# Cross-attention on one Trainium2 core: two subtractions change places, a normalization is halved, stores change queues and the end is put in another order

## The chip, the core and the metric

The kernel runs on one core of a Trainium2 chip. The core has TensorE (PE; its weight loads are shown as PEld), VectorE (DVE), ScalarE (ACT), GpSimd (POOL) and SyncE (SP), which here only issues DMAs. The metric is the device time of one execution in microseconds. A ratio of two kernels is after over before.

## The reference

For each of 32 batches a cross-attention of 512 queries over 77 keys, with 20 heads of 32 columns, then an output projection, a bias and the residual. The reference also has three further key ranges (4, 4 and 16 keys), which are empty, since the context has exactly 77 rows. What is left of it:

```python
q = _heads(hidden_states @ to_q_w)                    # x: (32, 512, 640)
h_txt = _sdpa(q, _heads(ehs_txt @ to_k_w), _heads(ehs_txt @ to_v_w))   # context: (32, 77, 1024)
out = _merge(h_txt) @ to_out_w + to_out_b + hidden_states
```

`_sdpa` is softmax(q k^T / sqrt(32)) v in float32.

## The kernel before

Every product is made of float32 halves: an operand is split into a high part (a cast to fp32r, done by ScalarE) and a low part (operand minus high part, done by VectorE or GpSimd), and a product is high x high + high x low + low x high. Each operand so costs a cast and a subtraction, and each product three matmuls (`PAIRS`).

**Phases.** Up to about 260 us the kernel projects the context of all batches to keys and values, in groups of 512 context rows (the last, `LAST`, has 416), and keeps both parts in DRAM (`k_dram`, `v_dram`). Then come 160 slots, `slot(n)`: 32 batches of five chunks of 128 columns (four heads each), n = 5 b + j with chunk j. Then `end()`. The order on each engine is the order in which the code issues instructions; no scheduler moves them. An instruction waits for what it needs, and everything behind it on its engine or queue waits with it.

**A slot, by what it does.** Work of several chunks lies in one slot. For chunk n: `scores(n, t)` for t = 0 to 3, a tile of 128 queries each (three matmuls into one of three PSUM banks `sc`, then `nm`, the negated maximum, by VectorE), and `exps(n, t)` by ScalarE (four exponentials into `pn`, each with its sum). For chunk n+1: `queries` (15 matmuls into `pq`) and `split_q` (ScalarE casts `qt`, GpSimd copies two halves to the other partitions, L458, VectorE makes the low parts, L460); the next slot's scores read all three. For chunk n-1: `sums` (reciprocals, L506), `normalize` (GpSimd multiplies `pn`, L511) and `transpose_p` (VectorE transposes to `z`, L518, and SP stores it to DRAM, L525). For chunk n-3: `load_p` (SP loads the transposed probabilities as `raw`, L534 and L535). For chunk n-4 (`taken`), the probabilities are split and used:

- `cast_p`: ScalarE's two casts of `raw` into `pp`, 64 rows (L542) and 128 rows (L543);
- `last_p`: GpSimd's subtraction for the 64-row part (L556);
- `rest_p`: VectorE's subtraction for the 128-row part (L549);
- `values`: six matmuls into the PSUM tile `pa` (L570); the third and fourth read what `last_p` makes, the fifth and sixth what `rest_p` makes. There is one `pa`, so it must be free;
- `sum_a`: ScalarE copies the upper half of `pa` to `aw` (L581), VectorE adds it (L583).

For chunk n-5: `high_a` (ScalarE's cast of the attention's result into `at`, L590) and `low_a` (VectorE's subtraction, L595, the last that reads `pa`). And `piece`: the output projection of an earlier batch, matmuls `po` (L613), two pieces a slot; in chunk 3 the first piece reads the `at` that the same slot makes, in chunk 4 too. `finish` adds the residual (L642) and lets SP store it; `add_bias` (GpSimd, L606) adds the bias to a loaded residual. `split_x` and `transpose_x` prepare the next batch's x, in chunks 0 to 3.

**Keys.** `load_keys` puts a batch's keys into `kb`; `copy_keys` (GpSimd, L423 and L424) copies two parts of it, in chunk 1 for the second group of chunks and in chunk 4 for the next batch's first.

**Order by engine in a slot of the steady state, around the change.** GpSimd: `copy_keys` (chunks 1 and 4 only), `last_p`, `normalize`, the two copies of `split_q`, `add_bias`, the low parts of `split_x`. VectorE: `nm`, the reciprocals, `nm`, `rest_p`, `low_a` (in chunk 4 `low_a` comes before the second `nm`), `nm`, `split_q`'s two, `nm`, `transpose_p`, the two additions of `sum_a`. ScalarE: `cast_p`, `high_a` (in chunk 4 the other way round), eight exponentials, the cast of `split_q`, four, the copy of `sum_a`, four. TensorE: scores, queries, scores, queries, scores, first piece, `values`, scores, second piece.

**First slots.** Slots 0 to 7 have no projection yet (`has_out` is false; a batch's output starts one batch later), slots 0 to 2 make the last group's values beside, and the first `raw` is loaded in slot 3 (`LATE`). `filling` delays the refills of keys and values to behind `load_p` in slots that take a chunk but have no projection.

**The queue.** SP issues its DMAs in order. Each one holds one of eight semaphores until it has landed, so the ninth waits for the first.

## Time and profile before

| | us |
|---|---|
| three timed runs | 1936.98 median (1931.66 to 1938.36) |
| the profiled execution | 1923.57 |
| its span | 1921.7 |
| slot 0 begins | 262.2 |
| slot 10 begins | 365.6 |
| slot 159, the last, begins | 1864.3 |
| the last matmul ends | 1917.6 |

The steady state, in the order of costs, from the page's groups (line, engine, operation, out<-in, shapes, count, then busy time and mean ns of one, then the idle time of the engine before them and what ended most of it):

```profile
L549 DVE TENSOR_TENSOR pp<-raw,pp 128x1024 fp32r<-128x1024 f32 x160 | 261.1, 1632 | 31.0 <-ACT pp L543 24.9
L556 POOL TENSOR_TENSOR pp<-raw,pp 64x512 fp32r<-64x512 f32 x160 | 212.4, 1327 | 97.5 <-ACT pp L542 88.5
L511 POOL TENSOR_TENSOR pn<-pn,rs 128x1232 f32<-128x1232 f32 x160 | 503.5, 3147 | 23.8 <-DVE rs L506 12.3
```

A time in a timeline is that from the span's start; a row gives start, length, engine, line, operation, out<-in, shapes, how often in a run, and in brackets how long the engine was idle before it and what ended that.

### The profile page before, as it was taken

How to read it: one execution, taken by the hardware profiler on the slowest of the kernel's cores; microseconds unless marked ns; L12 is line 12 of the kernel's file. 1: busy time of each engine (PE TensorE's matmuls, PEld its weight loads, DVE VectorE, ACT ScalarE, POOL GpSimd, SP SyncE). 2: the span in 40 equal slices, each digit the busy share in tenths (PEclk: the TensorE clock that was granted, in tenths of full speed). 3: DMA queues.
4: the chain of work that ended last, by engine and by line, in shares of the span. 5: the costliest groups of instructions: out<-in, count | busy, mean ns of one | idle time of the engine just before them, and what ended most of it. 6: DMA issues, size and time to landing. Idle time of an engine off the chain costs nothing.

```text
span 1921.7 us, 37548 instructions
## 1 busy us (share of the span) xinstructions
PE 1883.1 (98%) x10332; PEld 1665.2 (87%) x10332; DVE 1626.7 (85%) x2494; ACT 1526.3 (79%) x6210; POOL 1422.3 (74%) x1116
## 2 busy tenths in 40 slices
PE   9999997999999999999999999999999999999998
PEld 7888886888888888888888889888888888888887
DVE  5444447899999989999999999999999999999985
ACT  3232247998998989899888899998998989999882
POOL 1100067888898888888888888888888888888873
PEclk9999998999999999999999999999999999999999
DMA  9878869898888888888989898898889888889875
GB/s 185 201 195 249 200 176 222 215 233 238 235 232 233 233 216 231 233 231 228 238 223 236 236 239 234 232 237 231 234 228 233 225 240 234 237 232 229 226 211 157
DMA packets 565022, 431.36 MB, mean 224 GB/s; under 512 B 191120, under 2 KB 473168, under 8 KB 564816
## 3 DMA queue, kind: packets, MB, share of 16 engines
q1 hardware_dynamic: 560304, 414.47, 84.0%
q0 software_dynamic: 4416, 14.34, 2.2%
q8 instruction: 85, 1.39, 0.3%
q14 instruction: 121, 0.99, 0.2%
q10 hardware_dynamic: 96, 0.16, 0.0%
HBM read 247.17 MB, written 181.64 MB: 223 GB/s over the span
## 4 chain that ended last, share of the span: by engine, by line
PE 44%; ACT 15%; DVE 14%; DMA 13%; issue 5%; SPq 5%; POOL 3%; DVEq 0%; POOLq 0%; ACTq 0%
PE pq L443 11%; PE po L613 11%; PE pv L191 6%; DMA raw<-pd 6%; ACT pn L496 6%; PE pk L191 6%; PE pa L570 5%; PE sc L478 4%; DVE pp L549 4%; DMA xs<-in_x_dram 3%; ACT pp L543 2%; DVE nm L486 2%; DVE z L518 2%; ACT xt L264 2%; ACT aw L581 2%
## 5 line engine op out<-in xcount | busy, mean ns | idle before, releaser
L496 ACT ACTIVATE pn<-sc,nm 128x77 f32<-128x77 f32 x2560 | 794.0, 333 | 32.6 <-DVE nm L486 27.7
L613 PE MATMUL po<-wo_s,at 128*128 128x320 f32 x3840 | 636.1, 314 | 7.3 <-DVE at L595 3.0
L443 PE MATMUL pq<-xt,wq_s 128*128 128x512 f32 x2400 | 621.4, 400 | 0.0
L613 PEld LDWEIGHTS po<-wo_s,at 128*128 128x128 f32 x3840 | 569.0, 189 | 15.9 <-DVE at L595 12.3
L496 ACT ACTIVATION_READ_ACCUMULATOR pn<-sc,nm 128x1 f32 x2560 | 545.7, 213 | 0.0
L511 POOL TENSOR_TENSOR pn<-pn,rs 128x1232 f32<-128x1232 f32 x160 | 503.5, 3147 | 23.8 <-DVE rs L506 12.3
L443 PEld LDWEIGHTS pq<-xt,wq_s 128*128 128x128 f32 x2400 | 429.9, 190 | 75.7
L478 PEld LDWEIGHTS sc<-kb,qt 128*128 128x128 f32 x1920 | 327.9, 189 | 59.7 <-POOL qt L458 12.1
L478 PE MATMUL sc<-kb,qt 128*128 128x154 f32 (+1 forms) x1920 | 317.9, 274 | 13.8 <-POOL qt L458 8.9
L486 DVE TENSOR_REDUCE nm<-sc 128x4 f32<-128x308 f32 x640 | 288.4, 451 | 44.1 <-PE sc L478 37.6
L549 DVE TENSOR_TENSOR pp<-raw,pp 128x1024 fp32r<-128x1024 f32 x160 | 261.1, 1632 | 31.0 <-ACT pp L543 24.9
L556 POOL TENSOR_TENSOR pp<-raw,pp 64x512 fp32r<-64x512 f32 x160 | 212.4, 1327 | 97.5 <-ACT pp L542 88.5
L570 PE MATMUL pa<-pp,vb 128*128 128x512 f32 x960 | 265.5, 407 | 10.0 <-DVE at L595 6.2
L518 DVE STREAM_TRANSPOSE z<-pn 128x1280 f32<-128x1280 f32 x160 | 241.9, 1512 | 8.0 <-DMA pd<-z 2.8
L583 DVE TENSOR_TENSOR pa<-pa,aw 64x512 f32<-64x512 f32 x320 | 222.7, 696 | 21.1 <-ACT aw L581 10.8
L460 DVE TENSOR_TENSOR qt<-pq,qt 64x512 fp32r<-64x512 f32 x320 | 219.2, 685 | 23.6 <-ACT qt L454 17.0
L265 POOL TENSOR_TENSOR xt<-xs,xt 128x512 fp32r<-128x512 f32 x160 | 202.6, 1292 | 34.0 <-ACT xt L264 30.7
L570 PEld LDWEIGHTS pa<-pp,vb 128*128 128x128 f32 x960 | 171.8, 190 | 57.8 <-DVE pp L549 13.2
L606 POOL TENSOR_TENSOR xr<-xr,bias 128x640 f32<-128x640 f32 x128 | 202.7, 1584 | 17.6 <-DMA xr<-in_x_dram 6.0
L458 POOL CAST qt<-qt 64x512 fp32r<-64x512 f32 x320 | 195.0, 609 | 21.7 <-ACT qt L454 2.0
L581 ACT COPY aw<-pa 64x1024 f32<-64x1024 f32 x160 | 161.9, 1012 | 47.5 <-PE pa L570 43.3
L542 ACT CAST pp<-raw 64x512 fp32r<-64x512 f32 x160 | 99.5, 622 | 97.6 <-DMA raw<-pd 97.3
(46 smaller groups left out, 1639.8 us busy)
## 6 DMA issues: line engine op xcount, KB each, us to landing
pd<-z SPq DMA_DIRECT2D x640, 160.0 KB, 3.5
raw<-pd SPq DMA_DIRECT2D x160, 512.0 KB, 4.0
xs<-in_x_dram SPq DMA_DIRECT2D x128, 320.0 KB, 7.2
xr<-in_x_dram SPq DMA_DIRECT2D x128, 320.0 KB, 3.8
out_dram<-xr SPq DMA_DIRECT2D x127, 320.0 KB, 3.7
raw<-pd SPq DMA_DIRECT2D x160, 128.0 KB, 4.2
v_dram<-vs SPq DMA_DIRECT2D x80, 192.0 KB, 4.1
k_dram<-ks POOLq DMA_DIRECT2D x20, 512.0 KB, 4.3
```

Source lines behind the costliest of these rows:

```text
L191: nc.tensor.matmul(held[j][:, :gn], w[:, k, a, :], cts[g, k][:, c, :gn], start=(k == 0 and n == 0), stop=(k == NK - 1 and n == 2),)
L443: nc.tensor.matmul(pqs[n], wq_s[:, k, a, j * P : (j + 1) * P], xts[b, k][:, c, :], start=(k == 0 and m == 0), stop=(k == NC_ - 1 and m == 2),)
L460: nc.vector.tensor_tensor(qt[r, 1 + w, :], pq[r], qt[r, 0, :].bitcast(F32), ALU.subtract)
L478: nc.tensor.matmul(sc[:, cols], qt[:, m, t * P : (t + 1) * P], keys_, start=(m == 0), stop=(m == 2),)
L486: nc.vector.tensor_reduce(nm, sc[:, :KCOLS].rearrange("p (h k) -> p h k", k=NKEY), AX.X, ALU.max, negate=True)
L496: nc.scalar.activation(pnb[n % 2][:, at, :NKEY], sc[:, i * NKEY : (i + 1) * NKEY], AF.Exp, bias=nm[:, i : i + 1], accum_out=sms[n][:, at : ...
L511: nc.gpsimd.tensor_tensor(pf, pf, rs.unsqueeze(2).to_broadcast([P, NQ * HPC, NKEY]), ALU.mult)
L518: nc.vector.transpose(z.rearrange("p b t j -> p t b j"), pn.rearrange("p (t h) k -> p t (h k)", t=NQ).rearrange("p t (b i) -> p t b i", i=Q),)
L549: nc.vector.tensor_tensor(pp[:, 2:4, :], raw[:, 0:2, :], pp[:, 0:2, :].bitcast(F32), ALU.subtract)
L570: nc.tensor.matmul(pas[n][:, p, :], vb[:, p, t, :], pp[:, c, :], start=(c == p), stop=(c == p + 2),)
L583: nc.vector.tensor_tensor(pa[64 * p : 64 * p + 64, 0], pa[:64, p], aw[:, p], ALU.add)
L613: nc.tensor.matmul(pos[b, t, h][:, :HALF], ats[b * NC_ + j][:, a, t * P : (t + 1) * P], wos[0][:, j, c, h * HALF : (h + 1) * HALF], start= ...
```

## The change

It has five parts, none of which adds or removes a matmul or a DMA.

1. `low_a` stands before `rest_p` on VectorE, in chunks 0 to 3 and in `end()`. In chunk 4 it already did.
2. `normalize` is two instructions, each on half of `pn`. In chunks 1 and 2, once there is projection work, it comes before `last_p`; elsewhere behind it. `copy_keys` comes behind `last_p` in every slot (it stood at the slot's start).
3. The reciprocals of chunks 4, 0 and 1 are taken at the end of their own slot, behind the last exponentials and ahead of the additions of `sum_a`, which is in two parts now (`copy_a`, `add_a`); elsewhere in the next slot as before.
4. The last group's 20 V stores go by SP's queue (they went by GpSimd's). In slots 1 to 7 the refills come behind `load_p` (they did from slot 4 on), and the bias is loaded in slot 5 instead of 3.
5. In slot 158 `values` comes ahead of the first piece. In `end()` a residual is loaded ahead of the values, one `add_bias` comes behind the turn that it stood before, piece 8 is five steps long and piece 9 three (four and four), and the last batch's projections are begun in other portions.

```diff
@@ split_values @@
-        engine = nc.gpsimd if g == LAST else nc.sync
         for i in range(HPC):
-            engine.dma_start(
+            nc.sync.dma_start(
@@ normalize @@
-        pf = pnb[n % 2][:, :, :NKEY]
-        nc.gpsimd.tensor_tensor(
-            pf, pf, rs.unsqueeze(2).to_broadcast([P, NQ * HPC, NKEY]), ALU.mult
-        )
+        half = NQ * HPC // 2
+        for k in range(0, NQ * HPC, half):
+            pf = pnb[n % 2][:, k : k + half, :NKEY]
+            nc.gpsimd.tensor_tensor(
+                pf, pf, rs[:, k : k + half].unsqueeze(2).to_broadcast([P, half, NKEY]), ALU.mult
+            )
@@ sum_a @@
-    def sum_a(n):
-        pa = pas[n]
-        aw = late[0].tile([64, 2, S], F32, tag="aw", name="aw", bufs=1)
-        nc.scalar.copy(aw, pa[64:])
+    def copy_a(n):
+        aws[n] = late[0].tile([64, 2, S], F32, tag="aw", name="aw", bufs=1)
+        nc.scalar.copy(aws[n], pas[n][64:])
+
+    def add_a(n):
+        pa, aw = pas[n], aws.pop(n)
         for p in range(2):
             nc.vector.tensor_tensor(pa[64 * p : 64 * p + 64, 0], pa[:64, p], aw[:, p], ALU.add)
+
+    def sum_a(n):
+        copy_a(n)
+        add_a(n)
@@ piece @@
     def piece(b, i):
-        for t, h, j in STEPS[CUTS[i] : CUTS[i + 1]]:
+        steps(b, CUTS[i], CUTS[i + 1])
+
+    def steps(b, i0, i1):
+        for t, h, j in STEPS[i0:i1]:
@@ slot @@
-        filling = taken is not None and not has_out
+        filling = n > 0 and not has_out
         if not filling:
             refill(b, j, 0)
         copied = {1: 1, 4: 0 if more else None}.get(j)
-        if has_out and copied is not None:
-            copy_keys(copied)
...
         s = scores(n, 0)
         if j == 2:
             finish()
-        rs = sums(n - 1) if n else None
+        if n and n - 1 not in rss:
+            rss[n - 1] = sums(n - 1)
+        if has_out and j in (1, 2):
+            normalize(n - 1, rss.pop(n - 1))
         if taken is not None:
             last_p(taken)
-        if not has_out and copied is not None:
+        if copied is not None:
             copy_keys(copied)
-        if n:
-            normalize(n - 1, rs)
+        if n - 1 in rss:
+            normalize(n - 1, rss.pop(n - 1))
         exps(n, 0, *s)
...
         s = scores(n, 1)
+        if j != NC_ - 1 and n - 1 in takes:
+            low_a(takes[n - 1])
         if taken is not None:
             rest_p(taken)
-        if j != NC_ - 1 and n - 1 in takes:
-            low_a(takes[n - 1])
-        if n == LATE:
+        if n == LATE + 2:
             nc.sync.dma_start(bias, bo.unsqueeze(0).to_broadcast([P, C]))
...
+        if n == N - 2:
+            values(taken)
         if has_out:
             if not early:
                 piece(bo_, first)
...
-        if taken is not None and not (early and j == 4):
+        if taken is not None and not (early and j == 4) and n != N - 2:
             values(taken)
...
         if taken is not None:
-            sum_a(taken)
+            copy_a(taken)
         for c in xsplits[1]:
             split_x(b + 1, c)
         exps(n, 3, *s)
+        if has_out and j in (4, 0, 1):
+            rss[n] = sums(n)
+        if taken is not None:
+            add_a(taken)
@@ end @@
         load_p(N - 3)
+        load_residual(last - 1, 3)
         load_values(last, 1)
-        load_residual(last - 1, 3)
...
         high_a(N - 5)
+        low_a(N - 5)
         last_p(N - 4)
         rest_p(N - 4)
         transpose_p(N - 1)
-        low_a(N - 5)
         add_bias(last - 1, 2)
-        add_bias(last - 1, 3)
...
         def turn(n):
             sum_a(n)
             cast_p(n + 1)
             high_a(n)
+            low_a(n)
             last_p(n + 1)
             rest_p(n + 1)
-            low_a(n)
 
         turn(N - 4)
+        add_bias(last - 1, 3)
         load_p(N - 1)
...
-        piece(last - 1, 8)
+        steps(last - 1, 32, 37)
         finish()
         values(N - 3)
-        piece(last - 1, 9)
+        steps(last - 1, 37, 40)
...
-        for i in range(4):
+        for i in range(3):
             begin(i, 0, 2)
         values(N - 2)
         turn(N - 2)
         for t in (0, 1, 3, 2):
             add_bias(last, t)
-        for i in range(4):
+        for i in range(3, 6):
+            begin(i, 0, 2)
+        for i in range(3):
             begin(i, 2, 3)
-        for i in (4, 5):
-            begin(i, 0, 3)
         take(N - 1)
+        for i in range(3, 6):
+            begin(i, 2, 3)
         for i in range(6):
             begin(i, 3, 4)
```

More of the change, by code (lines that the diff above doesn't have):

```diff
@@ L391 @@
     late = []
-    raws, pps, ats, pds, sms, pqs, pas, xrs, pos = ({} for _ in range(9))
+    raws, pps, ats, pds, sms, pqs, pas, xrs, pos, aws, rss = ({} for _ in range(11))
     bias = main.tile([P, C], F32, name="bias")
```

## The prediction, made before the result

> **What bounds the kernel now.** I read the page's busy times first, then TensorE's timeline, then the waits, then the other engines over slots 61 to 64. TensorE is busy 98% of the span at full clock, so only its waits can be won; an edit elsewhere counts only if TensorE waits for it.
>
> ```profile
> PE 1883.1 (98%) x10332; PEld 1665.2 (87%) x10332; DVE 1626.7 (85%) x2494; ACT 1526.3 (79%) x6210; POOL 1422.3 (74%) x1116
> ```
>
> A slot begins with three score matmuls. In TensorE's timeline slot 10 begins at 365.62 and slot 159 at 1864.26: 149 slots in 1498.64 us, 10.06 each. Slot 61 (880.48 to 890.33) has no wait: 9.85. So the steady state loses 0.21 a slot, 31 us in all, and five slots take 50.29 on average against 49.25. All waits, longest first, say for whom:
>
> ```profile
> PEld pa L570 <- DVE pp L549: 13.2, 29, 0.6
> PEld po L613 <- DVE at L595: 12.3, 29, 1.4
> PEld sc L478 <- POOL qt L458: 12.1, 13, 2.8
> PEld pa L570 <- DVE at L595: 10.2, 26, 1.8
> ```
>
> (Engine, tile and line that waited, for whom: us, times, longest.) There are 30 groups of five slots, so "29 times" is once a group. Slots 63 (chunk 3) and 64 (chunk 4) show the two regular ones, TensorE first, then VectorE, then GpSimd:
>
> ```profile
> 904.72 2.30 PE L613 MATMUL po<-wo_s,at 128*128 128x320 f32 x12
> 915.86 1.80 PE L570 MATMUL pa<-pp,vb 128*128 128x512 f32 x6
> 920.50 0.49 PE L478 MATMUL sc<-kb,qt 128*128 128x308 f32 x3
> ```
>
> ```profile
> 903.87 2.07 DVE L549 TENSOR_TENSOR pp<-raw,pp 128x1024 fp32r<-128x1024 f32 x1
> 905.87 0.68 DVE L595 TENSOR_TENSOR at<-pa,at 128x512 fp32r<-128x512 f32 x1
> 914.60 2.27 DVE L549 TENSOR_TENSOR pp<-raw,pp 128x1024 fp32r<-128x1024 f32 x1 [0.37 <-ACT pp L543]
> ```
>
> ```profile
> 913.86 0.57 POOL L424 CAST kb<-kb 64x462 fp32r<-64x462 f32 x1
> 914.51 1.28 POOL L556 TENSOR_TENSOR pp<-raw,pp 64x512 fp32r<-64x512 f32 x1
> 919.07 1.27 POOL L458 CAST qt<-qt 64x512 fp32r<-64x512 f32 x2
> ```
>
> Slot 63's projection takes 2.30 where 1.96 is usual (row at 894.85): its last three matmuls need low_a, done at 906.55. Slot 64's attention takes 1.80 for 1.57 (row at 886.79): its last two need rest_p. That rest_p lasted 2.07 and 2.27; free of last_p it takes 1.20 (row at 884.25). The excess is the time for which last_p ran: the two exclude each other.
>
> **The change, part by part.** No matmul is added or removed.
>
> *low_a ahead of rest_p (chunks 0 to 3).* In slot 63 high_a ends at 904.31 (ScalarE's row 903.73, 0.58), so low_a can end at 904.99; the projection needs it at 904.72 + 9 x 0.148 = 906.05. The 0.34 goes. Elsewhere the attention's first four matmuls no longer wait behind both. What is late next is rest_p: it used to queue during last_p and got in as that ended (904.86); now it asks at 904.99, after normalize has begun.
>
> *normalize in halves.* 2.27 alone (row at 331.76), so 1.14 a half, and one more gap between GpSimd instructions, 0.07 (914.51 + 1.28 to 915.87): 0.07 to 0.13 a slot, I take 0.10. Two rows bound what a half does to rest_p. At 320.14 rest_p started 0.66 after a normalize (319.48) and took 2.69: held to its end. At 884.25 it started 0.04 after one (884.21) and took 1.20, while that normalize took 3.39. So rest_p loses between nothing and one half, 1.2. In chunk 3 the lead will be some 0.1 to 0.5, nearer the second row; with last_p no longer in its way in chunk 2, I take 0.25 later for what VectorE hands to ScalarE, over chunks 2 and 3 together (bounds -0.35 and +0.85).
>
> The Trainium skill, "SBUF — State Buffer", section "SBUF: two separate sides", says of the port pair that VectorE and GpSimd share that whoever starts first holds it for the whole instruction and the other fully blocks. The rows at 319.48 and 320.14 agree; those at 884.21 and 884.25 do not, since the later one went first. By the rule every late rest_p waits out its half, and the sum becomes that of the second rival; by the rows it is the one below.
>
> *normalize first in chunks 1 and 2, reciprocals sooner.* Five-slot count unchanged: the 0.23 reciprocals only move ahead of add_a, behind exponentials already done (ScalarE's last in slot 60 ends at 880.97, VectorE is free at 881.28). GpSimd fills waits it has anyway (1.81 at 882.32 for keys, 2.91 at 893.50 for a cast). I cost it at nothing: ScalarE's qt copy is the cover there, and if last_p came more than 1 us later in chunk 1, attention would wait for it.
>
> *copy_keys behind last_p.* In chunk 4 last_p no longer stands behind two copies: it can start when the 64-row cast ends (912.98 + 0.63) at 913.68 instead of 914.51. last_p then ends at 914.97 and rest_p, as now 1.08 behind it, at 916.05, not 916.87, and attention's 0.23 goes. But the copies, once under the wait for the cast, now follow rest_p. Slot 4 already has this order:
>
> ```profile
> 310.91 1.50 DVE L549 TENSOR_TENSOR pp<-raw,pp 128x1024 fp32r<-128x1024 f32 x1 [3.00 <-DMA pd<-z]
> ```
>
> ```profile
> 311.38 1.45 POOL L423 CAST kb<-kb 64x462 fp32r<-64x462 f32 x1
> 312.89 0.57 POOL L424 CAST kb<-kb 64x462 fp32r<-64x462 f32 x1
> 315.87 1.27 POOL L458 CAST qt<-qt 64x512 fp32r<-64x512 f32 x2
> ```
>
> ```profile
> 317.20 0.34 PE L478 MATMUL sc<-kb,qt 128*128 128x154 f32 x1 [0.33 <-POOL qt L458]
> ```
>
> The first copy takes 1.45, held by rest_p, and from rest_p's end (312.41) to the last qt cast's (317.14) it is 4.73. So slot 64's casts end at 916.05 + 4.73 + 0.10 = 920.88, against 920.34 now, and with the 0.25 from above at 921.13. The next slot's scores need them: the last score followed the cast by 0.06, the queries at 317.37 by 0.23; unhindered, queries begin 0.32 after the slot. So a cast later than 0.09 into the slot delays it. Slot 65 would begin at 920.50 - 0.34 - 0.23 = 919.93; it now in effect begins at 921.13 - 0.09 = 921.04, 0.54 later than before. Five such slots took 49.88 (870.62 to 920.50) and would take 50.42. The average of 50.29 holds 0.41 more, from raw loads that land late; TensorE waiting longer gives them that time back, and I leave 0.10. 50.52 - 50.29 = +0.23, times 29.8 groups: **+7 us** (bounds: -31, all waits gone; +25, with 0.85 for 0.25).
>
> *First slots.* SP is passed by 20 V stores, and keys and bias go behind the first raw load. Its cast is the long wait there:
>
> ```profile
> 309.31 0.62 ACT L542 CAST pp<-raw 64x512 fp32r<-64x512 f32 x1 [5.36 <-DMA raw<-pd]
> ```
>
> ```profile
> 302.69 0.38 SPq L534 DMA_DIRECT2D raw<-pd  x1
> ```
>
> Before it SP has four keys (297.71 to 302.12) and the bias; then it will have four V stores from 297.61, at 0.47 (its usual spacing) to 1.10 (those keys'): raw goes at 299.5 to 302.0, 0.7 to 3.2 sooner. I take 2.0. GpSimd's 2.54 to 2.58 per four V stores is freed, under the same wait. The first projections' waits, 1.02 for low_a (351.37) and 0.35 for last_p (361.57), go by the new orders: **-3.4** (bounds -6 and -1).
>
> *End.* TensorE's waits from slot 159 on are 1.36 and 0.17, 1.22, 1.21, 1.34, 0.43, 0.59 and 0.16: 6.5, and the granted clock of the last stretch is 0.90. low_a first takes the 1.22; add_bias behind the turn frees last_p from the 6.00 that GpSimd waits for the residual, so 2.55 goes. But the next chunk's raw is landed by SP's queue as before (the cast at 1893.67 waits 0.98 for it), and low_a after it, 1.56 + 0.59 + 0.68, can't end before 1896.5; attention starting then instead of at 1898.57 is 2.1, less 0.9 for six projection matmuls now behind it. Of the last waits 0.7 go. Attention ahead of projection in slot 158 waits about 1.0 for rest_p, half of it under the raw: -2.1 + 0.9 - 0.7 + 0.5 = **-1.4** (bounds -4 and +1).
>
> Sum: 7 - 3.4 - 1.4 = +2.2 on the profiled execution's 1923.57: 1925.8. The three timed runs' median is 1936.98, 1.0070 of that; 1925.8 x 1.0070 = **1939**, no change to speak of.
>
> **Rivals.** *The freed waits stay free.* For it: 35.7 us of weight-loader waits in three rows hang on just the two instructions moved. Against: the 0.15 between cast and scores at slot 65. If the casts are no later, five slots save 0.57, 17 us, with the ends 22: 1901.5, as a median 1915. *Slower: GpSimd's casts in chunk 4 become the bound by a longer chain.* rest_p, past its turn, waits out most of a half in chunks 2 or 3, ScalarE's exponentials slip, and with them chunk 4's cast, last_p, copies and qt casts: 0.75 for 0.25, another 0.5 x 29.8 = 15: 1954. For it: the 2.69; against: the 1.20. It decides from 0.4 on, where the sum passes 0.3%. *The V stores don't do what they say*, raw landing no sooner behind them: 2.0 back, 1941.
>
> **Numbers.** Mine 0.45, freed 0.23, longer chain 0.32; the V stores lie inside each. 0.3% (5.8 us) is about what can be told from none. Mine spreads over 1931 to 1947 by its bounds: 0.10 faster, 0.60 same, 0.30 slower. The freed case is faster but for 0.02, the long chain slower but for 0.02. Together faster 0.26, same 0.31, slower 0.43. The range leaves 0.11 at each side: half of the freed case below 1914, a third of the longer chain above 1957.
>
> **What would show it.** Chunk 3's projection at 1.96 and chunk 4's attention at 1.57: the freed waits. A wait of a slot's second and third scores for POOL qt once in five slots, 0.7 to 1.1 long: my chain. copy_keys in chunk 4 at 1.4 or more: the hold. rest_p of 1.6 to 2.3 beside a half of normalize in chunk 3: the slower rival; 1.20: mine. The first raw cast at about 307. If chunk 4's casts end before the slot does, I am wrong on the middle.

## The result, and the profile after

| | before | after |
|---|---|---|
| median of six runs, us | 1933.79 (1931.66 to 1938.36) | 1952.12 (1946.29 to 1959.19) |
| ratio, 95% interval | | 1.0089 (1.0063 to 1.0116) |
| profiled execution, us | 1923.57 | 1959.19 |
| its span, us | 1921.7 | 1957.4 |

The change makes the kernel slower by 0.9%, 18 us; the forecast was 1939, no change to speak of. The profile of before is quicker than all its timed runs and that of after is the slowest of its six. So the profiles, 35.6 apart, show twice the difference that the runs do: they are read below for where the time goes, the runs for how much.

First the busy times of the changed kernel, from its page:

```profile
PE 1899.0 (97%) x10332; PEld 1664.7 (85%) x10332; DVE 1634.8 (84%) x2494; ACT 1539.5 (79%) x6210; POOL 1398.4 (71%) x1256
```

VectorE is 8 us busier than before and GpSimd 24 us less (normalize 54 less and the V stores 13, since they left its queue; the first key copy, now beside rest_p, 50 more). TensorE issues the same matmuls as before; what it lost, it lost for the most part in waits. Of the view of all waits, those of TensorE and its weight loads (who waited, for whom: us, times, longest), then the one for raw:

```profile
PEld sc L477 <- POOL qt L457: 43.6, 72, 2.8
PEld pa L571 <- DVE pp L550: 30.2, 58, 1.0
PE sc L477 <- POOL qt L457: 26.8, 68, 2.5
PEld po L620 <- DVE at L602: 2.7, 7, 0.4
...
ACT pp L543 <- DMA raw<-pd: 72.7, 74, 4.2
```

The projection's wait for low_a, 12.3 before, is 2.7, and attention's for low_a, 10.2 before, is no longer among the longest. In their place the scores wait for the qt casts 72 times instead of 13, and attention waits for rest_p 58 times instead of 29. Slots 63 (chunk 3, from 918.35) and 64 (chunk 4, from 928.19) and the start of 65 show both, TensorE first:

```profile
922.88 1.96 PE L620 MATMUL po<-wo_s,at 128*128 128x320 f32 x12
...
933.80 1.94 PE L571 MATMUL pa<-pp,vb 128*128 128x512 f32 x6
...
938.58 0.31 PE L477 MATMUL sc<-kb,qt 128*128 128x308 f32 x1
939.22 0.34 PE L477 MATMUL sc<-kb,qt 128*128 128x154 f32 x1 [0.33 <-POOL qt L457]
939.89 0.34 PE L477 MATMUL sc<-kb,qt 128*128 128x154 f32 x1 [0.33 <-POOL qt L457]
```

Chunk 3's projection is down from 2.30 to its usual 1.96. Chunk 4's attention is not down: 1.94 for 1.80. Slot 65's second and third scores each wait for a qt cast; the slot lasts 10.99 in place of 9.83. VectorE and GpSimd in the same stretch say why:

```profile
923.01 0.69 DVE L602 TENSOR_TENSOR at<-pa,at 128x512 fp32r<-128x512 f32 x1 [0.99 <-ACT at L597]
923.61 1.74 DVE L550 TENSOR_TENSOR pp<-raw,pp 128x1024 fp32r<-128x1024 f32 x1
...
933.42 1.52 DVE L550 TENSOR_TENSOR pp<-raw,pp 128x1024 fp32r<-128x1024 f32 x1 [0.37 <-ACT pp L544]
```

```profile
921.68 1.29 POOL L557 TENSOR_TENSOR pp<-raw,pp 64x512 fp32r<-64x512 f32 x1 [0.70 <-ACT pp L543]
923.05 3.40 POOL L512 TENSOR_TENSOR pn<-pn,rs 128x616 f32<-128x616 f32 x2
...
932.57 1.29 POOL L557 TENSOR_TENSOR pp<-raw,pp 64x512 fp32r<-64x512 f32 x1 [0.64 <-POOL xt L264]
933.92 1.45 POOL L422 CAST kb<-kb 64x462 fp32r<-64x462 f32 x1
935.43 0.57 POOL L423 CAST kb<-kb 64x462 fp32r<-64x462 f32 x1
936.08 2.42 POOL L512 TENSOR_TENSOR pn<-pn,rs 128x616 f32<-128x616 f32 x2
938.56 1.27 POOL L457 CAST qt<-qt 64x512 fp32r<-64x512 f32 x2
```

In slot 63 VectorE does low_a, and when it comes to rest_p (923.61) normalize has been running for 0.56: rest_p takes 1.74 for 1.20. It ends 7.0 us into the slot instead of 5.76, the maxima behind it are late, ScalarE's exponentials with them, and so chunk 4's 64-row cast: over all groups its median start moves from 2.61 to 3.66 us into the slot. The lead is that long because low_a first waits for ScalarE's high_a (idle 0.99 in the row at 923.01), which ends 4.63 us into slot 63, against 4.12 before. In slot 64 GpSimd then runs without a gap from last_p to the second qt cast, which ends at 939.83, 1.25 after slot 65 has begun.

To compare kernels I took from each trace by how much successive matmuls start later than at their usual spacing, and summed it by place over 29 groups of five slots (slots 10 to 154), in us. A few hundredths a matmul are always in it, so about 1 a place is none. The last column is the mean of five slots.

| kernel | scores, ch. 0 | attention, ch. 1 and 2 | projection, ch. 3 | attention, ch. 3 | attention, ch. 4 | five slots |
|---|---|---|---|---|---|---|
| before | 0.1 | 11.8 | 9.2 | 3.5 | 9.0 | 50.32 |
| changed | 31.7 | 4.6 | 3.5 | 8.3 | 9.9 | 51.35 |
| e1_keys_first | 0.1 | 41.5 | 0.9 | 1.7 | 18.4 | 51.43 |
| e2_low_behind | 23.4 | 18.9 | 3.8 | 1.6 | 1.0 | 50.88 |
| e3_whole | 26.9 | 2.2 | 4.8 | 40.2 | 10.0 | 52.42 |
| e4_end_alone | 0.1 | 19.3 | 14.9 | 3.7 | 10.6 | 50.84 |
| e6_start_back | 30.9 | 1.7 | 4.8 | 6.3 | 9.8 | 51.23 |
| e7_keys_first_c4 | 0.1 | 6.0 | 1.5 | 8.9 | 27.6 | 50.83 |
| e8_c4_and_low3 | 0.1 | 10.2 | 21.1 | 3.3 | 12.7 | 50.78 |
| e9_copies_alone | 19.0 | 8.0 | 13.4 | 3.2 | 1.0 | 50.77 |
| e10_low3_behind | 25.4 | 2.4 | 4.9 | 1.9 | 1.0 | 50.44 |
| e11_copies_split | 0.7 | 10.7 | 7.1 | 2.8 | 1.0 | 49.98 |
| e13_combined | 7.3 | 6.6 | 13.7 | 2.9 | 1.0 | 50.30 |
| e14_two_slots_only | 4.3 | 7.4 | 28.4 | 4.1 | 1.0 | 50.81 |

The middle of e4_end_alone is the kernel before's: 50.32 and 50.84 are two executions of the same code. So the last column alone tells little. Of the places, the scores and both attentions of chunks 3 and 4 agree between the two (within 1.6), while attention in chunks 1 and 2 (11.8 and 19.3) and the projection (9.2 and 14.9) do not: there a difference of 6 or 7 us between two kernels is not told from none.

### The profile page after: what moved, and what is told of

It reads as the page before. It is cut to its first block, busy times and chain, and to the rows that moved or that the text cites. A ratio compares the mean times of both kernels' runs of the same rounds, so it can differ in the third digit from the quotient of the medians.

```text
span 1957.4 us, 37555 instructions
## 1 busy us (share of the span) xinstructions
PE 1899.0 (97%) x10332; PEld 1664.7 (85%) x10332; DVE 1634.8 (84%) x2494; ACT 1539.5 (79%) x6210; POOL 1398.4 (71%) x1256
## 4 chain that ended last, share of the span: by engine, by line
PE 25%; DMA 22%; DVE 18%; ACT 12%; SPq 8%; issue 8%; POOL 7%; POOLq 0%; DVEq 0%; ACTq 0%
DMA raw<-pd 8%; PE pk L191 7%; PE pv L191 6%; DMA pd<-z 6%; PE pq L442 5%; ACT pn L495 5%; DMA xs<-in_x_dram 4%; DVE z L519 4%; DVE pp L550 4%; PE po L620 4%; SPq L526 3%; DVE nm L485 3%; POOL pn L512 2%; DVE xs L256 2%; DVE qt L459 2%
## 5 line engine op out<-in xcount | busy, mean ns | idle before, releaser
L442 PE MATMUL pq<-xt,wq_s 128*128 128x512 f32 x2400 | 627.9, 401 | 0.2
L512 POOL TENSOR_TENSOR pn<-pn,rs 128x616 f32<-128x616 f32 x320 | 449.7, 1427 | 104.3 <-DVE rs L505 92.2
L477 PE MATMUL sc<-kb,qt 128*128 128x154 f32 (+1 forms) x1920 | 332.3, 276 | 36.3 <-POOL qt L457 26.8
L571 PE MATMUL pa<-pp,vb 128*128 128x512 f32 x960 | 268.1, 406 | 12.3 <-DVE pp L550 4.9
L557 POOL TENSOR_TENSOR pp<-raw,pp 64x512 fp32r<-64x512 f32 x160 | 205.9, 1287 | 87.5 <-ACT pp L543 52.9
L519 DVE STREAM_TRANSPOSE z<-pn 128x1280 f32<-128x1280 f32 x160 | 241.8, 1511 | 14.4 <-POOL pn L512 8.7
L459 DVE TENSOR_TENSOR qt<-pq,qt 64x512 fp32r<-64x512 f32 x320 | 218.6, 683 | 15.5 <-ACT qt L453 10.5
L544 ACT CAST pp<-raw 128x1024 fp32r<-128x1024 f32 x160 | 168.2, 1052 | 0.0
```

What stands on the lines that cost most here:

```text
L442: nc.tensor.matmul(pqs[n], wq_s[:, k, a, j * P : (j + 1) * P], xts[b, k][:, c, :], start=(k == 0 and m == 0), stop=(k == NC_ - 1 and m == 2),)
L459: nc.vector.tensor_tensor(qt[r, 1 + w, :], pq[r], qt[r, 0, :].bitcast(F32), ALU.subtract)
L477: nc.tensor.matmul(sc[:, cols], qt[:, m, t * P : (t + 1) * P], keys_, start=(m == 0), stop=(m == 2),)
L512: nc.gpsimd.tensor_tensor(pf, pf, rs[:, k : k + half].unsqueeze(2).to_broadcast([P, half, NKEY]), ALU.mult)
L519: nc.vector.transpose(z.rearrange("p b t j -> p t b j"), pn.rearrange("p (t h) k -> p t (h k)", t=NQ).rearrange("p t (b i) -> p t b i", i=Q),)
L571: nc.tensor.matmul(pas[n][:, p, :], vb[:, p, t, :], pp[:, c, :], start=(c == p), stop=(c == p + 2),)
```

## The experiments

Each was timed in five rounds against the kernel before on the same chip. The chips differ (the kernel before took 1935.4, 1936.9, 1919.4 and 1935.5 in the four sets), so only ratios are compared.

| run | of the change it has | ratio to before, 95% interval |
|---|---|---|
| e1_keys_first | all but: keys copied first, chunks 1 and 4 | 1.0142 (1.0118 to 1.0167) |
| e2_low_behind | all but: low_a behind rest_p | 1.0054 (1.0036 to 1.0073) |
| e3_whole | all but: normalize whole | 1.0283 (1.0260 to 1.0306) |
| e6_start_back | all but: the start | 1.0077 (1.0056 to 1.0099) |
| e7_keys_first_c4 | all but: keys copied first, chunk 4 | 1.0036 (1.0021 to 1.0051) |
| e8_c4_and_low3 | as e7, low_a behind rest_p in chunk 3 | 1.0005 (0.9990 to 1.0020) |
| e4_end_alone | the end | 0.9992 (0.9977 to 1.0008) |
| e9_copies_alone | the copies behind last_p | 0.9980 (0.9966 to 0.9994) |
| e10_low3_behind | all but: low_a behind rest_p in chunk 3 | 1.0045 (1.0030 to 1.0061) |
| e11_copies_split | the copies behind last_p, one of chunk 4's ahead | 0.9958 (0.9939 to 0.9977) |
| e13_combined | e10, copies split, start as before | 1.0018 (1.0001 to 1.0034) |
| e14_two_slots_only | e13, normalize whole, low_a behind rest_p in chunk 0 too | 1.0021 (1.0000 to 1.0042) |

My first theory was that of the prediction: the copies behind rest_p make the qt casts late. The rival was low_a ahead of rest_p.

**e1_keys_first.** Edit against the changed kernel:

```diff
+        if has_out and copied is not None:
+            copy_keys(copied)
         if taken is not None and j != NC_ - 1:
             cast_p(taken)
...
-        if copied is not None:
+        if not has_out and copied is not None:
             copy_keys(copied)
```

> The changed kernel, but GpSimd copies the keys (copy_keys in chunks 1 and 4) at the start of the slot again, ahead of last_p. Theory (the copies behind rest_p are what makes chunk 4's qt casts late): TensorE's wait for POOL qt at the start of chunk 0, 31 us of weight-loader and score waits over the steady state of the changed kernel's profile (1.05 a group of five slots), falls under 3 us; attention in chunk 4 may wait 0.2 to 0.3 a group again, 7 to 9 us. Five slots 50.2 to 50.5, time over before 0.995 to 1.002. Rival (low_a ahead of rest_p makes rest_p miss its turn in chunk 3 and everything on ScalarE slips): the wait at chunk 0 stays above 15 us and the ratio above 1.004.

The scores' wait went (31.7 to 0.1), and the time rose all the same. Slot 71 (chunk 1) shows where to, GpSimd and then TensorE:

```profile
994.72 0.43 POOL L422 CAST kb<-kb 64x308 fp32r<-64x308 f32 x1
998.70 0.44 POOL L423 CAST kb<-kb 64x308 fp32r<-64x308 f32 x1 [3.55 <-DMA kb<-k_dram]
999.23 3.38 POOL L512 TENSOR_TENSOR pn<-pn,rs 128x616 f32<-128x616 f32 x2
1002.69 1.26 POOL L557 TENSOR_TENSOR pp<-raw,pp 64x512 fp32r<-64x512 f32 x1
```

```profile
1004.01 1.20 PE L571 MATMUL pa<-pp,vb 128*128 128x512 f32 x4 [2.65 <-POOL pp L557]
```

In chunk 1 the second copy's keys land 4 us into the slot; normalize and last_p queue behind the copy that waits for them, and attention waits for last_p (40.6 us in chunk 1). The run undid two things at once, so its time says nothing of either; e7_keys_first_c4 took them apart.

**e2_low_behind.** In all chunks but 4 `rest_p` comes before `low_a` again:

```diff
-        if j != NC_ - 1 and n - 1 in takes:
-            low_a(takes[n - 1])
         if taken is not None:
             rest_p(taken)
+        if j != NC_ - 1 and n - 1 in takes:
+            low_a(takes[n - 1])
```

> The changed kernel, but low_a stands behind rest_p again in chunks 0 to 3. Theory (copies decide, low_a only adds): rest_p in chunk 3 begins about 0.9 to 1.5 sooner and chunk 4's 64-row cast 0.4 to 0.9 sooner, so the wait at the start of chunk 0 halves, from 1.05 to 0.4 to 0.7 a group (10 to 18 us less); but the projection in chunk 3 waits 0.34 a group for low_a again and attention in chunks 1 and 2 up to 0.2 more: in all -8 to +8 us, ratio to before 1.005 to 1.013. Rival (low_a decides alone): wait at chunk 0 under 0.2 a group, ratio under 1.003. Rival (low_a does nothing): wait unchanged, ratio 1.014 or more.

0.35% less than the changed kernel: low_a first costs, and it does not decide alone. Chunk 4's cast came 0.92 sooner (median 2.74 into the slot), but the scores' wait fell only to 0.81 a group, not to 0.4 to 0.7. Attention in chunk 2 now waited 15.6 us, for low_a of the same slot: the next attention needs the `pa` that low_a reads last. The projection's wait did not come back (3.8).

**e3_whole.** `half = NQ * HPC // 2` becomes `half = NQ * HPC`.

> The changed kernel with normalize in one instruction of 2.3 us instead of two halves of 1.14, in the same places. Theory by exclusion (an instruction that begins 0.5 us or more after the other engine's waits for its end): rest_p in chunk 3, which now begins 0.56 after a half and takes 1.74, is held by the whole, 2.5 to 2.9, chunk 4's casts slip by another 0.7 to 1.1 and the wait at chunk 0 grows from 1.05 to 1.7 to 2.1 a group: +15 to +30 us, ratio 1.017 to 1.025. Rival (halves cost gaps and hold nothing): 0.1 a slot saved on GpSimd, rest_p in chunk 3 unchanged, ratio 1.005 to 1.009.

VectorE and GpSimd in slot 63:

```profile
930.37 2.79 DVE L550 TENSOR_TENSOR pp<-raw,pp 128x1024 fp32r<-128x1024 f32 x1
```

```profile
929.80 2.28 POOL L512 TENSOR_TENSOR pn<-pn,rs 128x1232 f32<-128x1232 f32 x1
```

rest_p begins 0.57 after normalize and takes 2.79; behind a half, with the lead of 0.56, it took 1.74. The 1.05 between them is the whole's length less the half's (2.28 and 1.23): rest_p waits for the end of the instruction that runs, then needs 1.08 to 1.09. That part of the theory held. The place did not: attention in chunk 3 itself waited (40.2 us), the scores less than in the changed kernel (26.9 for 31.7, where more was expected), and it cost more than expected. Where low_a is first in chunk 3, the halves save 1.9%; where it is not, no gain of them shows (below, e14_two_slots_only).

**e6_start_back.**

```diff
+        engine = nc.gpsimd if g == LAST else nc.sync
...
-        filling = n > 0 and not has_out
+        filling = taken is not None and not has_out
...
-        if n == LATE + 2:
+        if n == LATE:
             nc.sync.dma_start(bias, bo.unsqueeze(0).to_broadcast([P, C]))
```

> The changed kernel with the start undone alone: the last group's V stores go by GpSimd again, keys and values are loaded where they were in the first slots, bias goes in slot 3. The first eleven slots of the changed kernel end 4.2 us later than before (369.80 for 365.62). Theory (the 16 to 20 V stores in SyncE's queue put the first raw load 1.3 us later, and the transposes behind it, instead of sooner): slot 10 begins 3 to 5 us sooner, time 2 to 5 us less, ratio to before 1.006 to 1.008. Rival (the first slots are late by the same moves as the steady state, or by chance): slot 10 begins within 1.5 us of the changed kernel's, ratio 1.008 to 1.011.

Slot 10 begins at 366.6, 3.2 sooner, as expected, but the 0.12% between the ratios lies within both intervals. All the profiles together say the same: slot 10 begins at 369.8 on average in the seven kernels with the new start (368.3 to 370.7) and at 367.3 in the seven with the old one (365.6 to 370.7). SP's queue and then ScalarE in the changed kernel:

```profile
298.20 3.04 SPq L526 DMA_DIRECT2D pd<-z  x4
301.34 2.58 SPq L234 DMA_DIRECT2D v_dram<-vs  x4
304.02 0.49 SPq L535 DMA_DIRECT2D raw<-pd  x1
```

```profile
310.11 0.62 ACT L543 CAST pp<-raw 64x512 fp32r<-64x512 f32 x1 [3.71 <-DMA kb<-k_dram]
```

The transposes' stores begin at 298.20 instead of 294.47: the transposes themselves end 2.4 later (296.45 for 294.05), and the queue, with the V stores in it, holds the stores another 1.3. From there raw goes 5.8 behind instead of 8.2, so the order in the queue does what was forecast. In e6_start_back raw goes later still, at 304.36, and is cast at 310.94, and yet slot 10 begins sooner: the first raw is not what the new start loses by. The slots' beginnings say where it does (means and extremes of the seven kernels with each start):

| us | new start | old start |
|---|---|---|
| slot 0 | 14.8 (14.2 to 15.5) | 13.5 (12.5 to 15.5) |
| slot 4, which waits for the first raw | 13.2 (12.6 to 15.0) | 14.4 (14.0 to 14.9) |
| slots 5 to 7 | 31.3 (31.0 to 31.9) | 29.3 (28.4 to 30.8) |

Slot 4 gains 1.2 and slots 5 to 7 lose 2.0 (31.4 in the changed kernel, 28.4 in e6, which differ in the start alone). Of what the start changes, the load of the bias now stands in slot 5; whether that is the cause no run shows.

**e7_keys_first_c4 and e8_c4_and_low3.** The first copies the keys at the slot's start in chunk 4 alone (`has_out and copied == 0`). The second does so too, and moves low_a behind rest_p where `j == 3`.

> The changed kernel, with the keys copied at the slot's start in chunk 4 alone; chunk 1 keeps the copies behind normalize and last_p. Theory (in chunk 4 the copies behind last_p are the cause of the wait; in chunk 1 copies first only made last_p wait for keys that had not landed): TensorE's wait for POOL qt at the start of chunk 0 falls from 31 us to under 3 as in the run with both undone, and attention in chunk 1 doesn't wait (40 us there, under 4 here); attention in chunk 4 waits 10 to 18 us in all. 15 to 30 us less than the changed kernel: ratio to before 0.992 to 1.000. Rival (the loss moves on to another wait of the same size, since GpSimd's work is as much as before and a little more): ratio above 1.003.

> The same and, in chunk 3 alone, low_a behind rest_p again. Theory (in chunk 3 low_a first makes rest_p come 0.56 after the first half of normalize has begun and wait for its end; behind last_p it goes in ahead of the half): rest_p in chunk 3 ends 1.2 sooner, chunk 4's cast 0.3 to 0.9 sooner, attention in chunks 3 and 4 waits 8 to 18 us less than with the copies alone, the projection of chunk 3 at most 6 us more: ratio to before 0.986 to 0.995. Rival (the projection's wait comes back in full and nothing else is won): ratio 0.2 to 0.5% above the run with the copies alone.

In e7 the scores' wait is gone, chunk 1 doesn't wait, and attention in chunk 4 waits 27.6 us: the ratio is the rival's. The copies cannot start before the three split_x subtractions that stand ahead of them, and last_p behind them ends 6.35 into the slot (5.71 in the changed kernel). In e8 the attention's waits fall as expected (36.5 to 16.0 in chunks 3 and 4), but the projection's wait for low_a comes back in full, 21.1: no faster than before, 0.3% faster than e7. Both ratios are above what I expected, by 0.4 and 0.6%. So the copies' place does not explain the loss. What they cost alone was the next question.

**e4_end_alone and e9_copies_alone.** The kernel before with one part of the change each: the new end; the copies behind last_p.

```diff
-        if has_out and copied is not None:
-            copy_keys(copied)
...
-        if not has_out and copied is not None:
+        if copied is not None:
             copy_keys(copied)
```

> The kernel before with the end of the changed kernel alone (attention first in slot 158, the turns, biases and projections of the end in the new order). The prediction has -1.4 us (bounds -4 and +1) for it; in the changed kernel's profile slots 158 and 159 together are 63.5 against 62.8. If the new order is worth what was forecast, the two take 61.4 and the ratio is 0.999; if it is worth nothing, 62.6 to 64, ratio 0.999 to 1.002. The middle is the kernel before's and shows how far its five slots (50.3 in the one profile) differ from one profile to another: 50.2 to 50.8.

> The kernel before with copy_keys behind last_p in chunks 1 and 4, and nothing else of the change. Theory (the copies alone put the qt casts of chunk 4 past the slot's end): last_p and rest_p of chunk 4 come 0.7 to 0.8 sooner, attention there doesn't wait (9 us to under 3), the last qt cast ends 10.4 to 10.6 after the slot's start instead of 9.97, and the next slot's scores wait 0.4 to 0.7 a group (12 to 20 us): ratio 1.001 to 1.007. Rival (the casts are only late because rest_p of chunk 3 made ScalarE late): no wait at chunk 0, ratio 0.994 to 0.999.

The end is worth nothing that can be measured. Slots 158 and 159 together take 62.7 to 63.1 in the three profiles with the old end and 62.6 to 63.99 in ten of the eleven with the new one (65.8 in e3_whole).

The copies alone make the kernel 0.2% faster, though they do just what the theory says. GpSimd in slot 64 and the first scores of slot 65 of e9_copies_alone:

```profile
919.77 1.29 POOL L556 TENSOR_TENSOR pp<-raw,pp 64x512 fp32r<-64x512 f32 x1 [0.61 <-POOL xt L265]
921.12 1.45 POOL L423 CAST kb<-kb 64x462 fp32r<-64x462 f32 x1
922.63 0.57 POOL L424 CAST kb<-kb 64x462 fp32r<-64x462 f32 x1
923.28 2.27 POOL L511 TENSOR_TENSOR pn<-pn,rs 128x1232 f32<-128x1232 f32 x1
925.62 1.28 POOL L458 CAST qt<-qt 64x512 fp32r<-64x512 f32 x2
```

```profile
926.01 0.61 PE L478 MATMUL sc<-kb,qt 128*128 128x308 f32 x2
926.95 0.34 PE L478 MATMUL sc<-kb,qt 128*128 128x154 f32 x1 [0.33 <-POOL qt L458]
```

The scores wait 0.66 a group (0.4 to 0.7 expected; the forecast had 0.54), chunk 4's attention not at all. But the theory took the scores' wait for a loss on the whole, and the ratio says otherwise. Against the profile of e4 (the same middle as before) the scores lose 19 and all other places win 23; against the profile of before they win only 8, and which of the two is nearer to the timed runs the traces don't decide. Chunk 4's attention wins 8 to 10 against both. What pays for the rest of the scores' wait is not shown. The raw loads of chunks 1 to 3 don't show it: ScalarE's idle time ahead of their casts is 90 us, against 87 (before) and 100 (e4). My theory had the mechanism and the wrong sign.

**e10_low3_behind.** The changed kernel, with rest_p before low_a in chunk 3 alone.

> The changed kernel with one thing undone in one chunk: in chunk 3 low_a stands behind rest_p again; copies, halves, sums and all else stay. Theory (the change loses where rest_p of chunk 3 waits for the end of a half of normalize; the copies alone made the kernel 0.2% faster): rest_p of chunk 3 begins 1.0 to 1.2 sooner and takes 1.5 instead of 1.74, chunk 4's 64-row cast comes 0.5 to 0.8 sooner, the wait at the start of chunk 0 falls from 1.05 to 0.6 to 0.8 a group, attention in chunks 3 and 4 waits under 6 us together (18 now): ratio to before 0.997 to 1.003. Rival (normalize first in chunks 1 and 2 or the halves cost it): attention in chunks 1 to 4 waits as now and the ratio stays above 1.005.

The time halves its distance to before, 1.0089 to 1.0045, less than expected. The places went as said, but for the scores' wait, 0.88 a group where 0.6 to 0.8 was expected:

```profile
PEld sc L477 <- POOL qt L457: 38.0, 72, 2.7
...
PEld po L620 <- DVE at L602: 6.8, 14, 1.2
...
PEld pa L571 <- DVE pp L550: 3.8, 8, 1.0
```

rest_p of chunk 3 begins 1.4 sooner (median 3.95 into the slot), chunk 4's cast 0.76 sooner (2.90), attention in chunks 3 and 4 waits 2.9 in place of 18.2 us. So low_a ahead of rest_p in this one chunk is worth some 0.44% of the time, about half of the loss, with an uncertainty of 0.3%. The rest is elsewhere.

**e11_copies_split.** The kernel before with the copies behind last_p, but the first of chunk 4's two ahead of the casts:

```diff
...
-        if has_out and copied is not None:
-            copy_keys(copied)
+        if has_out and copied == 0:
+            copy_keys(copied, (0,))
...
-        if not has_out and copied is not None:
-            copy_keys(copied)
+        if copied is not None:
+            copy_keys(copied, (1,) if has_out and copied == 0 else (0, 1))
```

> The kernel before with the copies behind last_p, but in chunk 4 one of the two copies (0.56) stays ahead of last_p, in the wait for the cast, and only the other stands behind it. Theory (the copies behind last_p win the attention's wait and lose at the next slot by the 2 us they put ahead of the qt casts; half of them fits into the wait): last qt cast of chunk 4 ends 0.6 to 1.4 sooner than with both behind, the wait at chunk 0 falls from 19 us to under 6, attention in chunk 4 waits under 4 us: ratio to before 0.990 to 0.997. Rival (ScalarE's and VectorE's chain through the five slots sets the pace, and what GpSimd gains appears as a wait for low_a or rest_p in chunks 1 to 3): those waits grow by 8 us or more, ratio 0.997 to 1.001.

0.42% faster than before, the best kernel of the study. GpSimd in its slot 64 and TensorE behind it:

```profile
908.45 0.56 POOL L424 CAST kb<-kb 64x462 fp32r<-64x462 f32 x1
909.09 1.28 POOL L558 TENSOR_TENSOR pp<-raw,pp 64x512 fp32r<-64x512 f32 x1
910.44 1.46 POOL L426 CAST kb<-kb 64x462 fp32r<-64x462 f32 x1
911.97 2.27 POOL L513 TENSOR_TENSOR pn<-pn,rs 128x1232 f32<-128x1232 f32 x1
914.31 1.28 POOL L460 CAST qt<-qt 64x512 fp32r<-64x512 f32 x2
```

```profile
915.51 0.49 PE L480 MATMUL sc<-kb,qt 128*128 128x308 f32 x3
```

One copy fits nearly whole under the wait for the cast (last_p starts 0.24 after the cast's end, 0.13 in e9_copies_alone), and the three scores run without a wait: the second cast ends at 915.59, 0.08 into the slot.

**e13_combined and e14_two_slots_only.** The first is e10 with the copies split as in e11 and the start as before the change; the second undoes the halves and low_a first in chunk 0 as well.

> The changed kernel with low_a behind rest_p in chunk 3, the copies of chunk 4 split as in the run before this one, and the start as before the change. Theory: normalize first with low_a first in chunks 1 and 2 takes 5 to 8 us of attention's waits away, the split copies take the wait at chunk 0 away: ratio to before 0.985 to 0.994, the fastest of all. Rival (the pace is set by the chain through ScalarE and VectorE): as the run with the split copies, within 0.2%, or slower for the halves' gaps.

> The combined run with two more things undone: normalize in one instruction, and low_a behind rest_p in chunk 0 as well as in chunk 3. Left of the change: the copies behind last_p (split), normalize first with low_a first in chunks 1 and 2, the sums sooner, and the end. Theory (what is left of the loss, 0.6% between the combined run and the run with the split copies, is chunk 0, where rest_p waits for a half as in chunk 3, 2.2 for 1.2, and the halves' gaps of 0.14 ahead of the qt casts): rest_p in chunk 0 takes 1.2 to 1.6, the wait at the start of chunk 0 falls from 7 us to under 3, ratio to before 0.993 to 0.998. Rival (normalize first in chunks 1 and 2 costs it, since last_p and rest_p come 0.7 to 1.0 later there): ratio 0.999 to 1.004.

Both were to be as fast as e11 or faster; they are 0.6% slower than it. In e14 rest_p of chunk 0 takes 1.21 as expected and the scores wait 4.3 (7.3 in e13; under 3 was expected), but the two ratios are the same: the halves and low_a first in chunk 0, undone together, bring nothing that can be told. What e14 has and e11 has not is normalize and low_a first in chunks 1 and 2, the sums sooner, and the end, which is worth nothing by itself. No run takes the first three apart. TensorE's longest wait of this kind is now chunk 3's for low_a; in e14 and, below it, in e11:

```profile
PEld po L623 <- DVE at L605: 27.6, 28, 1.4
```

```profile
PEld po L615 <- DVE at L597: 10.1, 21, 1.3
```

In e13, as slow as e14, this wait is 13.7 in the table, within what two profiles of the same code differ by, and the scores' is 6.6 more than in e11. The other engines show what moves, over 29 groups and in us into the slot. (e11 and e13 ran on one chip, e14 on another, on which the kernel before takes 0.8% longer.)

| | e11 | e13 | e14 |
|---|---|---|---|
| last_p of chunk 1 ends (median) | 3.92 | 4.82 | 4.80 |
| rest_p of chunk 1 ends (median) | 5.00 | 5.99 | 6.37 |
| rest_p of chunk 2 ends (median) | 5.56 | 6.56 | 6.84 |
| chunk 3: ScalarE ends the exponentials of the slot before (mean) | 2.07 | 2.73 | 2.84 |
| chunk 3: the 64-row cast of raw begins (mean) | 2.13 | 2.79 | 3.32 |
| chunk 3: ScalarE's idle time before that cast, all 29 together | 4 | 4 | 15 |

last_p is late since normalize stands ahead of it. rest_p is late for another reason: in chunks 1 and 2 it begins as low_a ends in all 58 slots of either kernel, and is then held by last_p in only 6 of them in e14 and 13 in e13. low_a in its turn begins in chunk 1 as high_a ends (0.03 behind, median). Two slots on ScalarE is 0.7 to 0.8 late with its exponentials. In e13 that is all of the cast's lateness; in e14 it is 0.77 of 1.19, and only there does raw that lands later add the rest. In e14's slot 63 the cast follows the last exponential without idle time:

```profile
910.62 0.21 ACT L498 ACTIVATION_READ_ACCUMULATOR pn<-sc,nm 128x1 f32 x1
910.80 0.62 ACT L546 CAST pp<-raw 64x512 fp32r<-64x512 f32 x1
```

high_a, low_a and with them chunk 3's projection stand behind that cast. That this chain is what costs the 0.6% is read from these rows; no run takes it alone. And taking low_a back in chunks 0 to 2 brought the changed kernel nothing: e2, with low_a behind in all four chunks, has 1.0054, e10, in chunk 3 alone, 1.0045. There rest_p came sooner (chunk 1's ends at 5.02 instead of 5.90), but attention in chunk 2 waited for low_a. So what of normalize, low_a and the sums costs the 0.6% stays open.

## Why the prediction was right or wrong

The range, 1914 to 1957, held the time, but only because it reaches into the second rival's case: by my own sum's bounds, 1931 to 1947, 1952 lies outside. The main forecast, 1939, was 13 us too low. The nearest case was that rival, the longer chain, with 1954. Its mechanism is one that the runs show; that its sum comes so near is partly luck, since it puts 15 us more on a step that e10 finds worth 8.5 in all, and nothing on the rest.

**Freed waits.** Chunk 3's projection: right, 9.2 to 3.5 us. Chunk 4's attention: wrong under this change, since its cast came later; with the copies alone 0.28 a group went (9.0 to 1.0 us), 0.23 forecast.

**The chain from rest_p to the qt casts.** Right: 4.73 + 0.10 forecast, 4.89 measured in slot 64 (934.94 to 939.83), the copy held to 1.45, the scores' two waits. The halves cost 0.15 (2.42 there, a whole 2.27 in e9_copies_alone) where I took 0.10.

**The failed step: "I take 0.25 later for what VectorE hands to ScalarE".** I expected a lead of 0.1 to 0.5 and took the row in which rest_p overtook; in the steady state the lead was 0.49 to 0.58 in all 29 slots of chunk 3, and rest_p took 1.72 to 1.81. Chunk 4's cast was to begin at 2.61 + 0.34 + 0.25 = 3.20 into the slot; it begins at 3.66. The lateness is thus 0.71, not 0.25, close to the rival's 0.75. My lead came from high_a's end in the profile of before; with the change high_a itself ends half a microsecond later in the slot. The rule of the Trainium skill, "SBUF — State Buffer", section "SBUF: two separate sides", that whoever starts first holds the shared port pair for the whole instruction and the other blocks, agrees with these 29 slots. For leads under 0.3 us it does not tell who goes first by the trace's starts (last section). By this sum 0.46 x 30 is 14 us, the size of the whole error, but e10_low3_behind, which takes the step back, gains only 0.44%, 8.5 us: the agreement of the 14 is chance, and the rest lies elsewhere.

**"I cost it at nothing": normalize first in chunks 1 and 2, reciprocals sooner.** Not borne out, but not pinned down either: with both, and low_a first there, the ratio is 1.0018 and 1.0021 (e13, e14), without them 0.9958 (e11). I named the qt copy as the cover and asked only whether attention would wait for last_p. It did not. rest_p came 1.0 to 1.4 later there, for the most part behind low_a, and ScalarE's exponentials behind it. Which of the three moves costs the time, and how much of it the changed kernel bears beside its other waits, no run shows.

**"TensorE waiting longer gives them that time back, and I leave 0.10".** Half right. Added to the kernel before alone, a wait of 0.66 a group did not make it slower (0.9980), so other waits shrank by as much; which, the traces don't decide. With the whole change the quickest five slots take 50.6 (50.42 forecast) and the mean 51.35, so 0.7 of lateness was still there in that execution.

**First slots.** The sum's sign was wrong: slot 10 began 2.5 us later on average, not 3.4 sooner. Raw went at 304.02, not at 299.5 to 302.0, and its cast ran at 310.11, not at 307, with the transposes ahead of it 2.4 late already. The term itself, 2.0 for a sooner raw, is there with 1.2 in slot 4; what I had no term for is the 2.0 that slots 5 to 7 lose.

**End.** -1.4 forecast, nothing that can be told from none measured, within its bounds.

The parts, each from its own pair of runs: copies -0.20%, low_a first in chunk 3 +0.44%, chunks 1 and 2 with normalize and low_a first, the sums and the end +0.63% (two chips), the start +0.12%, halves and low_a first in chunk 0 -0.03% (e13 less e14). They add to +0.96%, against +0.89% measured. Each has an interval of 0.15 to 0.3% at either side and its own surroundings, so the agreement is no proof; the start and the last are not told from none.

## What to carry to other kernels

When two engines exclude each other, moving an instruction ahead of one of them means asking what the other engine will have begun by then: with a lead of half a microsecond the whole rest of its instruction is the price, and shortening that instruction (the halves) limits it. An engine's wait for another is a place where work is free; fill it with as much as fits (one copy of two) and put only the remainder on the path. An order that delays nothing in its own slot can still cost: a late rest_p makes ScalarE late, and the rows of e13 and e14 suggest that TensorE pays for it two slots on.

## What the runs showed of the hardware

The hold is regular: where one of GpSimd's subtractions, multiplications or additions had begun 0.3 us or more earlier and had more than 0.1 us left, rest_p lasted what was left of it plus 1.08 to 1.09, in all 423 cases of five traces (before, changed, e3, e10, e14): 1.74 behind a half, 2.79 behind the whole, 1.52 behind last_p. (In 14 more cases GpSimd was within 0.1 us of its end, and rest_p took 1.20 to 1.22; alone it takes 1.20.) With shorter leads the lead does not tell who goes first. In the kernel before, in chunks 0 and 2, normalize had begun 0.11 to 0.12 earlier 40 times, and each time rest_p took 1.20 and normalize 3.45; in the changed kernel a half had begun 0.05 to 0.10 earlier 27 times, and each time rest_p waited, 2.23; in e3_whole a whole 0.13 to 0.18 earlier 30 times, rest_p 3.2; in e14 a whole 0.09 to 0.24 earlier 25 times, and rest_p went first in 23 of them (1.21). What decides there stays open.
